# Layer 0 of a four-layer graph network: the reciprocal softmax sums reach the query axis by a VectorE block transpose and transfers through DRAM instead of a TensorE product

## The chip, the cores and the metric

The kernel runs on one core of a Trainium2 chip. A core has TensorE (PE: products; its weight loads are listed as PEld), VectorE (DVE), ScalarE (ACT), GpSimd (POOL), SyncE (SP, which here only starts transfers) and 16 DMA engines. The metric is device time in microseconds of one launch; a case's time is the median over runs.

## The reference

Four layers on 4096 nodes with 256 features, each followed by a residual sum and a layer norm over the features. `adj` is 4096 x 4096, under 1% filled.

```python
# layer 0: four heads of 64
qkv = x @ Wqkv + bqkv
scores = einsum('hnd,hmd->hnm', qh, kh) * SCALE + graph_bias * adj
scores = where(adj == 0, -1e9, scores)
attn = softmax(scores, axis=-1)
x = layernorm(x + (attn @ vh) @ Wout + bout)
# layer 1: graph attention, softmax over leaky_relu(e_src + e_dst), masked
# layer 2: normalised adjacency @ x @ W.T + b;  layer 3: the same form, then relu
```

The change concerns the softmax of layer 0 alone: its division by the row sums.

## The kernel before

Layer 0 works on blocks of 128 query rows (`Rows`, 32 of them), and in each on two pairs of heads (`Pair`), so 64 pairs ("units"). The 4096 keys of a pair are taken in four steps of 1024. A step is written out by hand in `step(t)`: every engine gets its instructions in that order, and three units are in flight at different stages.

In one step, `t`, and for the units that are at that point:

- `score` (L366): TensorE writes scores of both heads into two PSUM tiles `sc`, 128 queries on the partitions, 1024 keys along. VectorE adds the bias and the mask, takes the row maximum and writes `z` (L375). There is one `sc` tile for each head, so the next step's scores wait until VectorE has read them.
- `expo` (L391), one unit (four steps) later: ScalarE takes the exponential of `z` with the row maximum subtracted, and accumulates the row sums into `ls`, one column for each step.
- `turn` (L405, L413), one step after that: TensorE transposes `z` in pieces into PSUM (`ptr`), ScalarE copies it to `pt`, keys now on the partitions.
- `attend` (L423), one step later still: TensorE accumulates values times `pt` into `po`, over the four steps. `po` is 128 x 128: the two heads' 64 features on the partitions, the queries along. It takes one of two PSUM buffers by turns.

Because `po` has the queries along its columns while the sums have them on the partitions, one reciprocal for each query and head must be laid along the columns, the same for the 64 partitions of its head. `sums` (L434 to L437), in the third of a pair's four attending steps, adds the four partial sums, takes the reciprocal and copies each along 64 columns (`lb`, 128 x 128). `norm` (L441 to L449), in the fourth, multiplies `lb` as the stationary operand with the identity on TensorE, which gives `lb` transposed in PSUM (`pb`), and VectorE copies it to `rb`. `scale` (L452), at the head of the next step, multiplies `po` by `rb` into `oT`; on VectorE it stands ahead of that step's two `z`. After a second pair, `finish` (L335 to L348) multiplies `oT` with the output weights, adds the residual and takes the layer norm's statistics.

Beside this, VectorE builds the next block's bias from the adjacency (`make_bias`: `rt` L272, `u` L277, `bias` L278), and ScalarE and GpSimd keep a bf16 copy of it (`make_edges`: `mk` L289; on a diagonal piece two small GpSimd operations L293, L294; GpSimd starts the transfer to `edge` in DRAM, L295). `mk` has two buffers. The query projection of the next block (`begin`: `pq` L313, and GpSimd's addition to `xr`, L329) stand in the step that begins with a second pair's `scale`. SP starts the loads of `raw` (L256), `xq` and `xr`.

Each engine works through its own instructions in order, and a wait stops all that stands behind it on that engine. GpSimd's starts of transfers are such instructions too.

Of the kernel before, what the change touches and what calls it, by code (L numbers as in the profile page):

```python
# [8 lines left out]
F32 = mybir.dt.float32  # L9
# [7 lines left out]
P = 128  # L17
# [3 lines left out]
HD = D // H  # L21
NCH = N // P
# [4 lines left out]
NS = N // TS  # L27
# [3 lines left out]
QB = P // NA  # L31
# [13 lines left out]
def tile_gnn(  # L45
# [18 lines left out]
    nc = tc.nc  # L64
# [8 lines left out]
    dram = ctx.enter_context(tc.tile_pool(name="dram", bufs=1, space=DRAM))  # L73

    ident = const.tile([P, P], F32, name="ident")
# [29 lines left out]
    sc = [ps_q.tile([P, TS], F32, name=f"sc{j}") for j in range(2)]  # L105

    edge = dram.tile([N, N], BF16, name="edge")
    off_diag = const.tile([P, P], F32, name="off_diag")
    nc.vector.tensor_scalar(off_diag, ident, -1.0, 1.0, ALU.mult, ALU.add)

# [58 lines left out]
    with ExitStack() as l0:  # L169
        ps_t = l0.enter_context(tc.tile_pool(name="l0ps_t", bufs=1, space=PSUM))  # L170
        ps_o = l0.enter_context(tc.tile_pool(name="l0ps_o", bufs=1, space=PSUM))
# [5 lines left out]
        wk2 = l0.enter_context(tc.tile_pool(name="l0work2", bufs=2))  # L177
# [26 lines left out]
        def project(mb):  # L204

            xt = x_in.pop(mb)
            for pr in range(2):
                pk = ps_o.tile([P, 512], F32, tag=f"po{pr}", name="pk")
                for cc in range(2):
                    nc.tensor.matmul(  # L210
                        pk,
                        wkv_sb[:, cc, pr * P : (pr + 1) * P],
                        xt[:, cc, :],
                        start=(cc == 0),
                        stop=(cc == 1),
                    )
                nc.scalar.activation(
                    kT[:, pr, mb * 512 : (mb + 1) * 512],
                    pk,
                    AF.Identity,  # L220
                    bias=bqk_sb[:, 2 + pr : 3 + pr],
                )
            pv = ps_t.tile([P, 4, D], F32, tag="tr", name="pv")
            for s in range(4):
                for cc in range(2):
                    nc.tensor.matmul(  # L226
                        pv[:, s, :],
                        xt[:, cc, s * P : (s + 1) * P],
                        wkv_sb[:, cc, D : 2 * D],
                        start=(cc == 0),  # L230
                        stop=(cc == 1),
                    )
            nc.vector.tensor_tensor(
                v_sb[:, mb * 4 : (mb + 1) * 4, :],
                pv,
                bv_b.unsqueeze(1).to_broadcast([P, 4, D]),
                ALU.add,
            )
            if mb + 4 < N // 512:
                load_x(mb + 4)  # L240
# [109 lines left out]
        class Pair:  # L350
# [79 lines left out]

            def sums(self):

                l2 = wk2.tile([P, 2], F32, tag="l2", name="l2")
                nc.vector.tensor_reduce(l2, self.ls, AX.X, ALU.add)  # L434
                nc.vector.reciprocal(l2, l2)
                self.lb = wk2.tile([P, 2, HD], F32, tag="lb", name="lb")
                nc.vector.tensor_copy(self.lb, l2.unsqueeze(2).to_broadcast([P, 2, HD]))  # L437

            def norm(self, tag):
                pb = ps_o.tile([P, 512], F32, tag=tag, name="pb")  # L440
                nc.tensor.matmul(  # L441
                    pb[:, 0:P],
                    self.lb.rearrange("p j d -> p (j d)"),
                    ident,
                    start=True,
                    stop=True,
                )
                self.rb = wk2.tile([P, P], F32, tag="rb", name="rb")
                nc.vector.tensor_copy(self.rb, pb[:, 0:P])  # L449

            def scale(self):
                nc.vector.tensor_tensor(  # L452
# [4 lines left out]
        pairs = {}  # L457
# [4 lines left out]
        def step(t):  # L462
            unit, k = divmod(t, NS)
            ib, pr = divmod(unit, 2)
            live = t < n_steps
            ua, ka = divmod(t - LA, NS)
            tag_a, tag_o = f"po{ua % 2}", f"po{1 - ua % 2}"
            ut, kt = divmod(t - LT, NS)
            ue, ke = divmod(t - LE, NS)
            attends = 0 <= ua < n_units  # L470
            turns = 0 <= ut < n_units
            expos = 0 <= ue < n_units
            grow = live and ib + 1 < NCH
            if grow and pr == 0 and k == NS - 1:
                rows[ib + 1].fetch()
            if ua > 0 and ka == 0:
                pairs[ua - 1].scale()
            if t > 0:
                for mb in range(2 * t, min(2 * t + 2, N // 512)):
                    project(mb)  # L480
            if live:
                if k == 0:
                    pairs[unit] = Pair(rows[ib], pr)
                pairs[unit].score(k)
            if expos:
                pairs[ue].expo(ke, 0)
            if turns:
                pairs[ut].turn(kt, 0)
            if expos:
                pairs[ue].expo(ke, 1)  # L490
            if attends:
                pairs[ua].attend(ka, tag_a)
                if ka == NS - 2:
                    pairs[ua].sums()
                if ka == NS - 1:
                    pairs[ua].norm(tag_o)
            if ua > 0 and ka == 1:
                if ua % 2 == 0:
                    pairs[ua - 1].rows.finish(tag_o)
                del pairs[ua - 1]  # L500
            if grow:
                if pr == 1 and k == NS - 2:
                    rows[ib + 1].begin(tag_o if attends else "po1")
                kb, half = divmod(pr * NS + k, 2)
                if edges:
                    edges.pop().make_edges()
                edges.append(rows[ib + 1])
                rows[ib + 1].make_bias(kb, half)
                if half == 0 and kb + 1 < NS:
                    rows[ib + 1].load(kb + 1)  # L510
                elif half == 0 and ib + 2 < NCH:
                    rows[ib + 2].load(0)
            elif edges:
                edges.pop().make_edges()
            if turns:
                pairs[ut].turn(kt, 1, by_dve=not live)
            for f, *args in tail.get(t, ()):
                f(*args)

# [131 lines left out]
        with tc.manual_schedule():  # L651
            load_x(0)
            nc.sync.dma_start(wkv_sb, wqkv[:, D:].rearrange("(c p) e -> p c e", p=P))
            rows[0].load(0)
            load_x(1)
            rows[0].load(1)
            rows[0].fetch()
            load_x(2)
            load_x(3)
            nc.scalar.dma_start(wout_sb, wout.rearrange("(c p) e -> p c e", p=P))  # L660
            nc.scalar.dma_start(bout_b, bout.partition_broadcast(P))
            rows[0].begin("po1")
            for k in range(NS):
                for half in range(2):
                    rows[0].make_bias(k, half)
                    rows[0].make_edges()
                if k < 2:
                    project(k)
                if k + 2 < NS:
                    rows[0].load(k + 2)  # L670
                elif k + 2 == NS:
                    rows[1].load(0)
            for t in range(n_steps + LA + 2):
                step(t)
# [5 lines left out]
    with ExitStack() as l1:  # L680
        wk = l1.enter_context(tc.tile_pool(name="l1work", bufs=2))
        pp_ = l1.enter_context(tc.tile_pool(name="l1pt", bufs=2))
        ps_o = l1.enter_context(tc.tile_pool(name="l1ps_o", bufs=2, space=PSUM))
# [166 lines left out]
    with ExitStack() as l2:  # L850
# [173 lines left out]
        with tc.manual_schedule():  # L1024
            prepare(0, 0)
            sums(0)
            prepare(1, 0)
            blk = None
            for t in range(n_all):
                layer, tl = divmod(t, T1)  # L1030
                jb, c = divmod(tl, NP)
# [4 lines left out]
                if t + 1 < n_all:  # L1036
                    sums(t + 1)
# [8 lines left out]
                if c == NP - 1:  # L1046
# [8 lines left out]
                    for s in range(NSJ):  # L1055
                        p = jb * NSJ + s
# [65 lines left out]
```

## Time and profile before

| | us |
|---|---|
| runs, median of 3 | 2810.7 (2809.99 to 2813.46) |
| profiled execution | 2810.3 |
| its span, first to last instruction | 2808.5 |
| TensorE busy | 2740.4 (98%) |
| VectorE busy | 2234.3 (80%) |
| ScalarE busy | 1615.1 (58%) |
| GpSimd busy | 234.2 (8%) |

Layer 0 fills about the first 1435 us of the span, layer 1 ends near 1990, and layers 2 and 3 fill the rest. The kernel-wide shares are means over these stages. A row of the list of groups reads: line, engine, operation, output <- inputs, shapes and count, then busy time in all and mean duration in ns of one, then the engine's idle time just before these instructions and what ended it. Instructions on TensorE overlap, so what one adds is read from the chain that ended last, in which each piece is what the next had to wait for.

### The profile page before, as it was taken

The numbers are of one execution on the slowest core, as the hardware profiler recorded it, in microseconds if no ns is written. First come the engines' busy times: TensorE is split into PE (matmuls) and PEld (weight loads), VectorE is DVE, ScalarE is ACT, GpSimd is POOL, SyncE is SP. The second block draws the span as 40 slices with busy tenths as digits, with TensorE's granted clock in tenths as the row PEclk, the third lists the DMA queues.
The fourth block names the chain that finished last, engine by engine and source line by source line (L and its number), as shares of the span: only waits on it lengthen the run. The fifth ranks groups of instructions, "written<-read, shape, count | busy, mean of one in ns | idle before, by whom it ended". The sixth has DMA issues, their size and how long they took to land.

```text
span 2808.5 us, 58032 instructions
## 1 busy us (share of the span) xinstructions
PE 2740.4 (98%) x23664; PEld 1870.2 (67%) x23664; DVE 2234.3 (80%) x4091; ACT 1615.1 (58%) x2483; POOL 234.2 (8%) x404
## 2 busy tenths in 40 slices
PE   6999999999999999999998999999999999999997
PEld 4677777777777777777777888887444444444443
DVE  4799999999898999999758888885876568666565
ACT  2699999999999999999855655653100001000000
POOL 1111111111111111111100000000200000000000
PEclk9999999999999999999998999999999999999999
DMA  6344444444444444444362222212555545555552
GB/s 157 61 86 85 87 92 85 88 86 88 90 87 82 90 91 82 86 92 89 100 188 68 76 73 70 76 46 72 177 157 173 163 154 163 164 160 179 180 169 76
DMA packets 671291, 308.01 MB, mean 110 GB/s; under 512 B 547376, under 2 KB 577456, under 8 KB 671024
## 3 DMA queue, kind: packets, MB, share of 16 engines
q1 hardware_dynamic: 655776, 265.10, 38.4%
q0 software_dynamic: 13440, 37.77, 3.5%
q8 instruction: 185, 3.03, 0.5%
q10 hardware_dynamic: 1808, 1.44, 0.2%
q14 instruction: 82, 0.67, 0.1%
HBM read 258.21 MB, written 46.01 MB: 108 GB/s over the span
## 4 chain that ended last, share of the span: by engine, by line
PE 96%; DVE 2%; ACT 1%; DMA 1%; issue 1%; SPq 0%; DVEq 0%; ACTq 0%
PE m L950 27%; PE po L423 17%; PE po L775 16%; PE sc L366 16%; PE ptr L405 10%; PE py L984 2%; PE pq L313 1%; PE pp L335 1%; PE pb L441 1%; PE pk L210 1%; PE pv L226 1%; PE sc L137 1%; PE pm L744 0%; SPq L256 0%; DMA xt<-in_xT 0%
## 5 line engine op out<-in xcount | busy, mean ns | idle before, releaser
L375 DVE CUSTOM_DVE_ANT_0 z<-sc,bias 128x1024 f32<-128x1024 f32 x512 | 605.8, 1220 | 40.5 <-PE sc L366 38.9
L391 ACT ACTIVATE z<-z,nm 128x1024 f32<-128x1024 f32 x512 | 590.2, 1153 | 6.7 <-DVE nm L387 6.7
L413 ACT COPY pt<-ptr 128x1024 f32<-128x1024 f32 x507 | 511.3, 1008 | 99.2 <-PE ptr L405 89.3
L366 PE MATMUL sc<-store,qT 64*128 64x512 f32 x2048 | 507.0, 608 | 1.4 <-DVE mx L375 1.3
L423 PE MATMUL po<-pt,xc 128*64 128x128 f32 x8192 | 504.1, 276 | 0.0
L775 PE MATMUL po<-store,pt 128*128 128x257 f32 x2048 | 459.5, 382 | 3.6 <-DVE pt L765 3.6
L423 PEld LDWEIGHTS po<-pt,xc 128*64 128x64 f32 x8192 | 442.1, 137 | 17.6 <-DVE pt L411 0.2
L405 PEld LDWEIGHTS ptr<-ident,z 64*128 64x128 f32 x8192 | 322.3, 138 | 177.6 <-issue 78.4
L775 PEld LDWEIGHTS po<-store,pt 128*128 128x128 f32 x2048 | 385.0, 190 | 62.9 <-issue 3.6
L950 PE MATMUL m<-asum,ysum 128*128 128x512 f32 x768 | 357.0, 595 | 6.3 <-issue 6.3
L405 PE MATMUL ptr<-ident,z 64*128 64x64 f32 x8192 | 356.5, 225 | 5.8 <-ACT pt L413 4.4
L366 PEld LDWEIGHTS sc<-store,qT 64*128 64x128 f32 x2048 | 192.9, 189 | 119.7 <-issue 109.4
L950 PEld LDWEIGHTS m<-asum,ysum 128*128 128x128 f32 x768 | 146.1, 190 | 177.9 <-issue 160.2
L950 PE MATMUL m<-asum,store 128*128 128x512 f32 x512 | 263.1, 596 | 0.0
L724 ACT ACTIVATE z<-z,es_q 128x1024 f32<-128x1024 f32 x128 | 147.1, 1149 | 183.2 <-DVE mx L711 178.9
L950 PE MATMUL m<-a,ysum 128*128 128x512 f32 x512 | 245.3, 592 | 0.0
L295 POOL DMA_DIRECT2D edge<-mk x256 | 145.3, 568 | 1004.5 <-ACT mk L289 981.0
L956 ACT COPY e<-m 128x512 f32<-128x512 f32 x32 | 18.5, 586 | 351.3 <-PE m L950 351.3
L919 DVE TENSOR_TENSOR asum<-a 128x512 f32<-128x512 f32 x128 | 88.0, 687 | 163.7 <-PE m L950 163.7
L278 DVE SCALAR_TENSOR_TENSOR bias<-rt,gb,u 128x512 f32<-128x512 f32 x256 | 194.1, 758 | 9.1
L950 PEld LDWEIGHTS m<-asum,store 128*128 128x128 f32 x512 | 97.8, 191 | 123.6 <-issue 121.9
L272 DVE STREAM_TRANSPOSE rt<-raw 128x512 f32<-128x512 f32 x256 | 179.6, 702 | 0.0
(126 smaller groups left out, 2544.5 us busy)
## 6 DMA issues: line engine op xcount, KB each, us to landing
a<-in_adjT SPq DMA_DIRECT2D x256, 512.0 KB, 5.1
raw<-in_adjT SPq DMA_DIRECT2D x512, 128.0 KB, 3.9
edge<-mk POOLq DMA_DIRECT2D x256, 128.0 KB, 2.5
mk<-edge SPq DMA_DIRECT2D x256, 128.0 KB, 2.9
xt<-in_xT SPq DMA_DIRECT2D x8, 512.0 KB, 5.3
xq<-in_xT SPq DMA_DIRECT2D x32, 128.0 KB, 3.8
xr<-in_x SPq DMA_DIRECT2D x32, 128.0 KB, 3.0
x<-xs POOLq DMA_DIRECT2D x8, 512.0 KB, 4.0
```

Of the source, the lines that this page charges most:

```text
L272: nc.vector.transpose(rt.rearrange("p (b r) -> p b r", r=QB), self.raw_now[:, half * nb : (half + 1) * nb, :],)
L278: nc.vector.scalar_tensor_tensor(self.bias[k][:, m0 : m0 + HT], rt, gb, u, ALU.mult, ALU.add)
L295: nc.gpsimd.dma_start(edge[self.ib * P : (self.ib + 1) * P, k * TS + m0 : k * TS + m0 + HT], mk)
L366: nc.tensor.matmul(ps[j][:, q * 512 : (q + 1) * 512], self.rows.qT[j * HD : (j + 1) * HD, self.pr, :], kT[j * HD : (j + 1) * HD, self.pr, ...
L375: nc.vector.tensor_tensor_reduce(z, ps[j], self.rows.bias[k], 1.0, NEG, ALU.add, ALU.max, self.mx[:, j, k : k + 1],)
L391: nc.scalar.activation(z, z, AF.Exp, bias=self.nm[:, j : j + 1], accum_out=self.ls[:, j, k : k + 1],)
L405: nc.tensor.transpose(pa[:, r, c, :], z[half, c * P : (c + 1) * P], ident[half, half])
L413: nc.scalar.copy(to, pa)
L423: nc.tensor.matmul(self.po[j * HD : (j + 1) * HD, 0:P], v_sb[:, ci, h * HD : (h + 1) * HD], self.pt[j][k][:, c, :], start=(ci == 0), stop= ...
L724: nc.scalar.activation(self.z[s], self.z[s], AF.Prelu, bias=self.eq[:, s : s + 1], alpha=SLOPE)
L775: nc.tensor.matmul(self.po[:, 0 : D + 1], self.pt[:, b, :, :].rearrange("p s i -> p (s i)"), wh[:, b, :], start=(b == 0), stop=(b == NBK - 1),
L950: nc.tensor.matmul(self.m[i], left, right, start=(c == 0), stop=(c == NP - 1))
```

## The change

`sums` now ends with a VectorE transpose in blocks of 32 x 32: the two reciprocals of each query are repeated to 32 columns, and after the transpose each block of 32 partitions holds head 0's 32 reciprocals on its even rows and head 1's on its odd rows. For each head GpSimd then starts a transfer of one row from each of the four blocks (four rows of 128 bytes) into a new DRAM tensor `norm`. A new function, `spread`, at the end of the same step, has GpSimd start two transfers that read 512 bytes each into 64 partitions of `rb`. The old `norm` function, with the TensorE product and the copy out of PSUM, is gone, and so is its call in the fourth attending step. `scale` is unchanged and reads `rb`.

```diff
+    norm = dram.tile([2 * NCH, 2, P], F32, name="norm")
             def sums(self):
+                u = 2 * self.rows.ib + self.pr
                 l2 = wk2.tile([P, 2], F32, tag="l2", name="l2")
                 nc.vector.tensor_reduce(l2, self.ls, AX.X, ALU.add)
                 nc.vector.reciprocal(l2, l2)
-                self.lb = wk2.tile([P, 2, HD], F32, tag="lb", name="lb")
-                nc.vector.tensor_copy(self.lb, l2.unsqueeze(2).to_broadcast([P, 2, HD]))
-
-            def norm(self, tag):
-                pb = ps_o.tile([P, 512], F32, tag=tag, name="pb")
-                nc.tensor.matmul(
-                    pb[:, 0:P],
-                    self.lb.rearrange("p j d -> p (j d)"),
-                    ident,
-                    start=True,
-                    stop=True,
-                )
+                lt = wk2.tile([P, QB], F32, tag="lt", name="lt")
+                nc.vector.transpose(lt, l2.unsqueeze(1).to_broadcast([P, QB // 2, 2]))
+                for j in range(2):
+                    nc.gpsimd.dma_start(
+                        norm[u, j, :].rearrange("(a c) -> a c", c=QB),
+                        lt.rearrange("(a r) c -> a r c", r=QB)[:, j, :],
+                    )
+
+            def spread(self):
+                u = 2 * self.rows.ib + self.pr
                 self.rb = wk2.tile([P, P], F32, tag="rb", name="rb")
-                nc.vector.tensor_copy(self.rb, pb[:, 0:P])
+                for j in range(2):
+                    nc.gpsimd.dma_start(
+                        self.rb[j * HD : (j + 1) * HD, :], norm[u, j, :].partition_broadcast(HD)
+                    )
...
                 if ka == NS - 2:
                     pairs[ua].sums()
-                if ka == NS - 1:
-                    pairs[ua].norm(tag_o)
...
             if turns:
                 pairs[ut].turn(kt, 1, by_dve=not live)
+            if attends and ka == NS - 2:
+                pairs[ua].spread()
```

The order of instructions that results: on VectorE the transpose takes the place of the copy `lb`, and the copy `rb` is gone. On GpSimd the two starts of writes stand ahead of the same step's `edge` transfer, and the two starts of reads behind it, each behind a wait for its write to have landed. `scale` waits for both reads and for `po`.

## The prediction

> **What bounds the kernel now.** I read the chain that ended last first, then busy time by stretch, then the same chain in order of time, then the groups of the touched lines, the order of work around one turn of the sums, and the transfers.
>
> ```profile
> PE m L950 27%; PE po L423 17%; PE po L775 16%; PE sc L366 16%; PE ptr L405 10%; PE py L984 2%; PE pq L313 1%; PE pp L335 1%; PE pb L441 1%; PE pk L210 1%; PE pv L226 1%; PE sc L137 1%; PE pm L744 0%; SPq L256 0%; DMA xt<-in_xT 0%
> ```
>
> The product that goes, `pb`, is itself on the chain, at 1%. In the middle of layer 0 (columns: PE, PEld, DVE, ACT, POOL busy, then clock, DMA share, GB/s):
>
> ```profile
> 500.00:700.00 200.00, 200.00 (x2848) 150.99 (x2844) 183.07 (x357) 186.92 (x309) 30.65 (x54) 1.00 0.44 88
> ```
>
> TensorE has no gap; ScalarE (93%) and VectorE (92%) are close behind. The chain in order of time, around one `pb`:
>
> ```profile
> 635.55 1.77 PE sc L366 x8
> 637.32 0.49 PE ptr L405 x16
> 637.81 1.90 PE po L423 x32
> 639.71 0.42 PE pb L441 x2
> 640.13 0.64 PE ptr L405 x16
> 640.77 1.77 PE sc L366 x8
> ```
>
> A step without `pb` is 1.77 + 0.49 + 1.90 + 0.64 = 4.80 us; this one is 5.22, longer by the 0.42 of `pb`. So the product is paid in full, once for each of 64 head pairs. A block of 128 rows (two pairs, eight steps) takes 41.58 us.
>
> The groups concerned:
>
> ```profile
> L441 PE MATMUL pb<-ident,lb 128*128 128x128 f32 x128 | 31.2, 326 | 0.0
> L449 DVE COPY rb<-pb 128x128 f32<-128x128 f32 x64 | 18.7, 292 | 21.0 <-PE pb L441 18.1
> L437 DVE COPY lb<-l 128x128 f32<-128x128 f32 x64 | 14.5, 227 | 2.2
> L295 POOL DMA_DIRECT2D edge<-mk x256 | 145.3, 568 | 1004.5 <-ACT mk L289 981.0
> ```
>
> POOL is nearly idle: it waits for ScalarE's `mk`. The tightest turn, that of a first pair:
>
> ```profile
> 615.56 0.15 DVE L434 TENSOR_REDUCE l<-ls 128x2 f32<-128x8 f32 x1
> 615.95 0.23 DVE L437 COPY lb<-l 128x128 f32<-128x128 f32 x1
> 616.36 0.54 POOL L295 DMA_DIRECT2D edge<-mk  x1 [5.32 <-ACT mk L289]
> 620.53 0.29 DVE L449 COPY rb<-pb 128x128 f32<-128x128 f32 x1
> 622.60 0.28 DVE L452 TENSOR_TENSOR oT<-po,rb 128x128 f32<-128x128 f32 x1
> 622.94 1.23 DVE L375 CUSTOM_DVE_ANT_0 z<-sc,bias 128x1024 f32<-128x1024 f32 x1
> ```
>
> `scale` (`oT`) stands 7.04 us after the sum's start, and the `z` behind it empties the two score buffers that TensorE fills again in the next step. That gap must hold the new transfers. Nearest rows for them:
>
> ```profile
> edge<-mk POOLq DMA_DIRECT2D x256, 128.0 KB, 2.5
> x_pre<-xr SPq DMA_DIRECT2D x31, 128.0 KB, 2.0
> ```
>
> **What the Trainium skill says.** (1) "DMA: Bandwidth & Descriptors", section on the anatomy of one DMA on the SWDGE (gpsimd) path: about 2.0 us fixed plus bytes/436e3, mostly the write's receipt. The trace agrees: `edge` is 2.2 at the least and 2.5 in the median, the formula gives 2.3. (2) The same page, "Two DMAs through the same engine are not ordered": a dependent transfer must be issued after the first one's semaphore, so two fixed costs add. Nothing in this trace depends so on a POOL transfer within a step. (3) "SBUF — State Buffer", "Who interferes with whom": VectorE in a two-port mode and GpSimd lock each other out of a shared port pair. The trace agrees: `u` (L277) takes 426 ns, and 1456 where POOL's `xr` addition lies beside it; the `edge` issue goes from 542 to 692 ns beside `u`.
>
> **The change part by part.**
>
> TensorE: minus one fp32 product for each pair, 0.42 us on the chain x 64 = 26.9 us. The 0.42 is a difference of steps, so weight loads and start-up are in it. Nothing is added on TensorE.
>
> VectorE: minus `lb` 0.23 and `rb` 0.29, minus the wait for `pb` (21.0/64 = 0.33). Plus one transpose of 128x32: the rows for 512 and 1024 columns are 0.70 and 1.24, so 1.04 ns a column over 0.17; at 32 columns 0.20. Bounds: 0.17 to 0.23 (no dearer than `lb`). VectorE is 0.3 cheaper for each pair, and is not the bound, so I count nothing for it.
>
> POOL: plus four DMA issues for each pair. Its order becomes: two writes (wait for the transpose), `edge` of that step (waits for `mk`), two reads (each waits for its write to land), next `edge`. An issue costs 0.54 (L295); with fewer rows I take 0.5, bounds 0.3 and 0.7: 4 x 0.5 x 64 = 128 us on an engine busy 234 of 2808. Behind the writes waits `edge`, 1.1 us later than now: ScalarE needs that `mk` buffer two steps later (9.6 us), the transfer lands in 2.5 to 3.2, so that is free. Behind the reads waits the next `edge`, whose `mk` comes at 5.3 us; they are out before. At the end of layer 0 POOL's `x` stores start at 1437.8, some 8 us after the last pair's reads would. SP's queue gets nothing. About 64 KB of reads for each pair is nothing beside 88 GB/s at 44% share.
>
> The new wait: `scale` waits for both reads, and behind it on VectorE stand `z` for both heads and thereby TensorE's next scores. From the sum's start (0): sum, reciprocal and transpose to 0.60; POOL notices 0.28 later, as it does after `mk` (616.07 to 616.35): 0.88; writes issued at 0.88 and 1.40. A tiny write is not in the trace. From below 1.7 us (16 engines begin to report 1.8 after an `edge` issue), from above 3.2 (mean of `edge` where the raw loads run); I take 2.2, the least `edge`: 3.1 and 3.6. Reads issued at 3.2 and 3.7, 2.2 to 2.5 each: last one at 5.9 to 6.2.
>
> When is it needed? Without `rb` and its wait, the `z` pair that ends at 620.38 is followed by 1.91 us of `rt`, `u` and `bias`, so `scale` would come at 622.29, 6.73 after the sum's start. Half a microsecond of cover. A further 0.3 is free: in the step at 615.59 `z` starts 0.46 later than usual and TensorE loses 0.16. Past 7.0 us each microsecond of lateness is a microsecond of TensorE. The raw loads start at 6.0 in this phase, just after the reads. In a second pair the same chain is due at about 6.9, and the step after it has 1.1 us of query projection ahead of the next scores, so it has cover to about 8.4. The last pair's `scale` stands 2 us ahead of the output product; its lateness is hidden by the `ped` products.
>
> Other removals: the PSUM turn of `po` tags loses one user, and no product waited for it; nothing counted. Layers 1 to 3 are untouched and start earlier.
>
> Sum: the profiled span 2808.5 - 26.9 = 2781.6. The profiled execution was 2810.3 (1.8 outside the span), so 2783.4; the median of the runs is 0.4 higher: **2784**.
>
> **Rivals.**
>
> A, *the round trip is late, slower.* Place: `scale` of the first pairs, then of all. If each transfer takes 3.2 instead of 2.2 to 2.5, the writes land at 4.6, `rb` at 7.9, and the block loses about the 0.84 that it gained: that is the break-even. With 3.4 it is 8.3: first pairs lose 1.3, second ones still nothing, so 32 x (1.3 - 0.84) = +15 us, about 2826. For it: `edge` has means of 3.1 to 3.9 where raw loads run. Against: from 2 to 6 us after a first pair's sum the DMA engines are idle, and the tiny packets ask little of them.
>
> B, *part of the gain is eaten.* ScalarE's 186.9 of 200 us is 38.9 for a block, 4.86 a step, against plain steps of 4.80, of which there are now six, not four, in eight. If they fell to ScalarE's pace, 6 x 0.06 x 32 = 11 us are lost: 2795. Or the new issues meet `u` at the port pair and delay it by up to 0.4, which costs about 0.16 a step as measured above, 5 to 10 us: 2789 to 2794. For it: the engines are this close. Against: ScalarE's first copy of a step still waits for `ptr`.
>
> C, *no change*: the step is really held by ScalarE, and `pb` fills time in which TensorE would wait: 2811. Against: the `pb` step is longer by exactly `pb`.
>
> **How the numbers follow.** Forecast as worked out, own range 2779 to 2792: 0.70. B: 0.14, 2793 to 2805. C: 0.04. A: 0.09. Better than 2779 (the 0.16 at 615.59 goes as well, 5 us): 0.03. Within 0.2% (5.6 us) is what a measurement cannot tell from no change. Faster 0.70 + 0.14 + 0.03 = 0.87; same 0.04; slower 0.09. The range leaves out A, C, the far end of B and the best case, just under 0.2: 2779 to 2801.
>
> **What would show it.** Right: the first pairs' period and the second's each shorter by 0.42, a block at about 40.7 us, no `pb` on the chain, no idle VectorE time ahead of `oT`, writes landing in about 2 us, and the last read by 6.2 after the sum. Wrong: VectorE idle ahead of `oT` released by `rb`'s transfer, with score products waiting for `mx`; `ptr` waiting for ScalarE in plain steps; `u` far above 0.43; POOL issues well above 0.5.

## The result: no change that can be measured

Over twelve runs each, the kernel after takes 2812.76 us (2808.79 to 2819.4) and the kernel before 2812.5 (2809.99 to 2816.28): a ratio of 1.0004, 95% interval 0.9995 to 1.0013. The profiled execution took 2810.95 us with a span of 2808.9, against 2810.3 and 2808.5. The forecast was 2784, so about 29 us of expected gain are missing.

**The product is gone, as said.** The chain that ended last, by line, for the kernel after:

```profile
PE m L956 27%; PE po L781 16%; PE po L425 16%; PE sc L368 15%; PE ptr L407 10%; PE py L990 2%; PE pq L315 1%; PE pp L337 1%; PE pk L212 1%; PE pv L228 1%; DVE z L377 1%; PE sc L139 1%; DMA rb<-norm 1%; SPq L258 0%; PE pm L750 0%
```

No `pb` stands in it. In its place are VectorE's `z` and the new transfer `rb<-norm`, 1% each. The same chain in order of time (start, duration, what), around a pair's fourth attending step, in which `pb` used to stand behind `po`:

```profile
636.74 1.77 PE sc L368 x8
638.51 0.49 PE ptr L407 x16
639.00 1.90 PE po L425 x32
640.90 0.64 PE ptr L407 x16
641.54 1.77 PE sc L368 x8
```

From scores to scores this step is 4.80 us; with `pb` it was 5.22. Where `rb` came in time, the whole period of a pair (from its first `z` to the first `z` of the next pair) is 18.85 us after a first pair and 21.89 after a second, against 19.27 and 22.31 before: exactly 0.42 less each.

**But TensorE now has gaps.** Busy time in two stretches of layer 0 (columns: length; PE, PEld, DVE, ACT, POOL busy, each with its instructions; then clock, DMA share, GB/s):

```profile
300.00:500.00 200.00, 197.36 (x2752) 147.89 (x2750) 172.26 (x342) 181.22 (x302) 51.89 (x91) 0.98 0.43 86
500.00:700.00 200.00, 200.00 (x2868) 152.14 (x2866) 177.75 (x353) 188.14 (x313) 51.70 (x90) 1.00 0.46 93
```

In the first, TensorE stands for 2.6 us and its clock falls to 0.98. In the second it is busy throughout, since instructions on it overlap and a wait of some tenths shows only as fewer of them: 2868 in the trace against 2888 in the same stretch of the run without these waits (first experiment below). The groups of the touched lines show which engine waits first:

```profile
L297 POOL DMA_DIRECT2D edge<-mk x256 | 143.9, 562 | 586.6 <-ACT mk L291 572.1 <-POOL mk L296 8.9 <-ACT pt L415 2.7
L443 POOL DMA_DIRECT2D norm<-lt x128 | 74.7, 586 | 290.0 <-DVE lt L441 287.1 <-issue 2.8
L453 POOL DMA_DIRECT2D rb<-norm x128 | 69.3, 544 | 64.7 <-DMA norm<-lt 49.4 <-issue 15.2
L458 DVE TENSOR_TENSOR oT<-po,rb 128x128 f32<-128x128 f32 x64 | 18.4, 288 | 45.0 <-DMA rb<-norm 39.7 <-PE ptr L407 2.9 <-PE sc L368 2.3
L441 DVE STREAM_TRANSPOSE lt<-l 128x32 f32<-128x32 f32 x64 | 13.5, 212 | 2.4 <-DVE l L438 0.3
```

VectorE stands idle for 45.0 us ahead of `scale` (`oT`), 39.7 of it until the transfer into `rb` lands. And TensorE waits in turn. The waits of the body of layer 0 (120 to 1345 us: sum, times, longest):

```profile
DVE oT L458 <- DMA rb<-norm: 25.1, 17, 4.4
...
PEld sc L368 <- DVE mx L377: 12.3, 16, 2.7
...
PE sc L368 <- DVE mx L377: 4.7, 4, 2.6
```

The score products wait for `mx`, which VectorE writes with `z` behind `scale`. One late turn in order of time, that of a first pair (start, duration, engine, line, operation, and in brackets the idle time before it and what ended it):

```profile
616.11 0.16 DVE L437 TENSOR_REDUCE l<-ls 128x2 f32<-128x8 f32 x1
...
616.76 0.21 DVE L441 STREAM_TRANSPOSE lt<-l 128x32 f32<-128x32 f32 x1 [0.30 <-DVE l L438]
...
621.87 0.43 DVE L279 TENSOR_SCALAR u<-rt 128x512 f32<-128x512 f32 x1
622.34 0.75 DVE L280 SCALAR_TENSOR_TENSOR bias<-rt,gb,u 128x512 f32<-128x512 f32 x1
624.29 0.29 DVE L458 TENSOR_TENSOR oT<-po,rb 128x128 f32<-128x128 f32 x1 [1.21 <-DMA rb<-norm]
624.50 1.22 DVE L377 CUSTOM_DVE_ANT_0 z<-sc,bias 128x1024 f32<-128x1024 f32 x1
```

`bias` is done at 623.1, 7.0 us after the sum began; `rb` comes 8.1 after it, and `z` follows 1.2 late.

**How often.** In 35 of the 64 pairs `scale` waits at most 0.15 us. In the other 29 it waits by the trace for 44.9 us in all. The table sorts them by what the trace shows late in each (pairs are counted from 0, so even numbers are first pairs). Its last column says by how much the period in which that `scale` stands is longer than in the run without these waits (first experiment below); for the last two blocks, all that is lost from pair 60 to the end of layer 0:

| what was late | pairs | VectorE idle, us | TensorE lost, us |
|---|---|---|---|
| GpSimd standing still for 2.8 to 2.9 us | 14, 29, 44, 59 | 12.2 | 11.0 |
| the second write landing in 3.2 to 3.7 us | 2, 12, 22, 32, 42, 52 | 7.6 | 5.1 |
| reads started 4.3 us after the sum, behind `edge` | 21, 23, 25, 27, 54, 56, 58 | 6.6 | 2.7 |
| a read landing in 3.5 to 4.0 us | 4, 11, 24, 31 | 4.8 | 1.9 |
| the last two blocks, where layer 1's loads begin | 60, 61, 63 | 12.3 | 6.7 |
| small ones | 7, 16, 43, 46, 50 | 1.4 | 0.3 |

In pair 54, the costliest of its row (2.7 us idle, 2.3 lost), the second read also took 4.5 us to land, so its late start is the smaller part.

### The profile page after: what moved, and what is told of

Read it like the earlier page. It is cut to its first block, busy times and chain, and to the rows that moved or that the text cites. A ratio compares the mean times of both kernels' runs of the same rounds, so it can differ in the third digit from the quotient of the medians.

```text
span 2808.9 us, 58279 instructions
## 1 busy us (share of the span) xinstructions
PE 2732.3 (97%) x23536; PEld 1864.5 (66%) x23536; DVE 2193.2 (78%) x4027; ACT 1608.2 (57%) x2483; POOL 378.9 (13%) x660
## 4 chain that ended last, share of the span: by engine, by line
PE 92%; DVE 3%; DMA 2%; issue 1%; ACT 1%; SPq 0%; POOL 0%; DVEq 0%; ACTq 0%; POOLq 0%
PE m L956 27%; PE po L781 16%; PE po L425 16%; PE sc L368 15%; PE ptr L407 10%; PE py L990 2%; PE pq L315 1%; PE pp L337 1%; PE pk L212 1%; PE pv L228 1%; DVE z L377 1%; PE sc L139 1%; DMA rb<-norm 1%; SPq L258 0%; PE pm L750 0%
## 5 line engine op out<-in xcount | busy, mean ns | idle before, releaser
L368 PE MATMUL sc<-store,qT 64*128 64x512 f32 x2048 | 521.7, 608 | 8.3 <-DVE mx L377 8.1
L407 PEld LDWEIGHTS ptr<-ident,z 64*128 64x128 f32 x8192 | 328.8, 138 | 177.1 <-issue 86.3
L407 PE MATMUL ptr<-ident,z 64*128 64x64 f32 x8192 | 366.4, 226 | 4.0 <-ACT pt L415 2.7
L368 PEld LDWEIGHTS sc<-store,qT 64*128 64x128 f32 x2048 | 200.6, 189 | 133.4 <-issue 105.4
```

Of the source, the lines that this page charges most:

```text
L368: nc.tensor.matmul(ps[j][:, q * 512 : (q + 1) * 512], self.rows.qT[j * HD : (j + 1) * HD, self.pr, :], kT[j * HD : (j + 1) * HD, self.pr, ...
L407: nc.tensor.transpose(pa[:, r, c, :], z[half, c * P : (c + 1) * P], ident[half, half])
```

## The experiments

Each was timed together with the kernel before on one chip; ratios are against that, with 95% intervals. "Forecast" below is the 2784 us on record.

### The whole gain, and what takes it away

The first question is whether the removal is worth what was forecast at all, if nobody waits for the new transfers. Two kernels answer it. In one every transfer stays, but `scale` uses the tile of the pair before, which has long landed:

```diff
+                self.rb_old = last_rb[-1] if last_rb else self.rb
+                last_rb.append(self.rb)
...
-                    self.rows.oT[:, self.pr, :], self.po[:, 0:P], self.rb, ALU.mult
+                    self.rows.oT[:, self.pr, :], self.po[:, 0:P], self.rb_old, ALU.mult
```

> The changed kernel with all its transfers, but each scale multiplies by the rb of the pair before, which landed some 15 us earlier (so the normalisation is that of the wrong pair). Theory W (the gain is lost where VectorE waits for rb ahead of z): the wait is gone, so the whole 0.42 us for each pair appears, 2784 to 2788 us, ratio about 0.991. Theory S (the transfers, GpSimd's four more issues and the port pair cost time by themselves): 2800 to 2812, ratio 0.996 to 1.000.

Measured: 2780.62 us (2780.14 to 2785.75), ratio 0.9895 (0.988 to 0.991). In the other the transpose and all four transfers are left out, and a constant tile of ones takes the place of `rb`:

```diff
-                lt = wk2.tile([P, QB], F32, tag="lt", name="lt")
...
-                    self.rows.oT[:, self.pr, :], self.po[:, 0:P], self.rb, ALU.mult
+                    self.rows.oT[:, self.pr, :], self.po[:, 0:P], rb_one, ALU.mult
...
-            if attends and ka == NS - 2:
-                pairs[ua].spread()
```

> The turn of the sums left out: no product, no transpose, no transfer, scale multiplies by a constant 1 (so nothing is normalised). This is the ceiling of what removing the product can bring. Forecast of the prediction: 64 x 0.42 = 27 us, 2784. Theory A (ScalarE takes over as the bound when the product goes): 2795 to 2811. If this is 2784 and the kernel with the old rb as well, the transfers cost nothing but their wait.

Measured: 2784.85 us (2781.21 to 2788.21), ratio 0.9905 (0.9889 to 0.9922). Both lie where the forecast lay. The first one's windows (columns as above) show a TensorE without gaps although GpSimd starts all the transfers:

```profile
300.00:500.00 200.00, 200.00 (x2876) 151.16 (x2872) 179.85 (x353) 189.49 (x316) 53.76 (x94) 1.00 0.44 91
500.00:700.00 200.00, 200.00 (x2888) 152.34 (x2884) 179.05 (x354) 189.28 (x313) 53.91 (x94) 1.00 0.46 94
```

So the transfers as such show no cost, ScalarE does not hold the step, and what the kernel after lost it lost by waiting for `rb`. That the kernel that leaves more out is the slower of the two by 4 us has little to do with layer 0. The first product that stands behind layer 0's output (`sc`, L139 in the kernel after) starts at 1407.8 us in the first run and at 1408.6 in the second, against 1435.0 in the kernel before. The other 3.7 us between the two profiled spans lie behind it, in layers 1 to 3, where the two kernels are alike.

Pair by pair against the first run, the kernel after loses 21.3 us over pairs 0 to 59: 19.3 in first pairs and 2.0 in second ones. What a pair loses follows from when its `rb` lands, in us after the sum's start:

| pair | `rb` lands | TensorE lost |
|---|---|---|
| 16, first | 6.8 | 0.0 |
| 22, first | 7.5 | 0.5 |
| 12, first | 8.3 | 1.3 |
| 54, first | 9.3 | 2.3 |
| 14, first | 10.9 | 7.1 |
| 21, second | 7.7 | 0.0 |
| 59, second | 8.9 | 0.5 |
| 29, second | 9.6 | 1.1 |

A first pair loses what `rb` comes later than 7.0, a second one what it comes later than 8.4. Only 15 of the 60 pairs are past these times, and the rule gives some 17 of the 21.3 us; 3.2 of the rest are pair 14's (last section). From pair 60 to L139 another 6.7 us are lost. Of the 30.2 us between the two spans 2.8 lie in layers 1 to 3; the kernel after was 0.6 ahead at its first sum.

### How much later may `scale` stand

Here `scale` stands behind the two `z` of its step instead of ahead of them, so a late `rb` does not stop the `z` for which the next scores wait:

```diff
-            if ua > 0 and ka == 0:
-                pairs[ua - 1].scale()
...
                 pairs[unit].score(k)
+            if ua > 0 and ka == 0:
+                pairs[ua - 1].scale()
```

> The changed kernel with scale moved on VectorE from ahead of the step's two z to behind them: 2.4 us more for rb to arrive, nothing else. Theory W: of the pairs that were late in the profile of the changed kernel only those late by over 2.4 us (7 of 64, four of them in the last block) still wait, and they wait where TensorE has its next scores already; 2785 to 2792 us, ratio 0.990 to 0.993. Theory S: no better than the changed kernel, 2808 to 2813.

Measured: 2800.39 us (2800.05 to 2801.61), ratio 0.9962 (0.9947 to 0.9977): some 11 us won, not the 19 to 26 expected. The waits in the body of layer 0:

```profile
PEld pq L315 <- DVE oT L458: 16.4, 30, 1.1
...
PE pq L315 <- DVE oT L458: 9.1, 30, 0.9
...
DVE oT L458 <- DMA rb<-norm: 1.7, 1, 1.7
```

The waits for `rb` have gone from 25.1 us to 1.7. But in place of them the query projection `pq` waits in each of 30 blocks, because it needs the PSUM buffer that `scale` of the second pair frees. The period in which a second pair's `scale` stands grows from 21.89 us to 22.24 in the median, some 11 us in all. So the later place is free for first pairs alone.

### The standstills

GpSimd's own timeline in the kernel after, at pair 14 (columns as in the turn above):

```profile
405.70 0.59 POOL L443 DMA_DIRECT2D norm<-lt  x1 [5.41 <-DVE lt L441]
409.06 0.58 POOL L443 DMA_DIRECT2D norm<-lt  x1 [2.78 <-issue]
409.64 0.57 POOL L297 DMA_DIRECT2D edge<-mk  x1
410.20 0.61 POOL L453 DMA_DIRECT2D rb<-norm  x1
412.30 0.53 POOL L453 DMA_DIRECT2D rb<-norm  x1 [1.49 <-DMA norm<-lt]
```

Between the two writes GpSimd waits 2.78 us for nothing that the profile shows ("issue"). It had started 128 transfers; the same happens after 249, 370 and 491, every 121. If it came with the number of GpSimd's instructions, more of them would move it. So sixteen tiny fills are added for each pair:

```diff
                         self.rb[j * HD : (j + 1) * HD, :], norm[u, j, :].partition_broadcast(HD)
                     )
+                for i in range(16):
+                    nc.gpsimd.memset(pad[:, i : i + 1], 0.0)
```

> The changed kernel with 16 tiny memsets on GpSimd for each pair, behind the two reads. The changed kernel's GpSimd stands still for about 3 us with nothing to wait for at 409, 722, 1034 and 1344 us: every 15 pairs, which is every 232 to 236 GpSimd records, or every 120 of its transfers. Theory F (it waits for its next instructions to be fetched, a fixed number at a time): now about 33 records a pair instead of 16, so a standstill every 7 to 8 pairs. Theory R (the ring of transfers is refilled): still every 15 pairs. Time 2805 to 2820 either way.

Measured: 2816.19 us (2810.36 to 2819.97), ratio 1.0012 (1.0005 to 1.0019). GpSimd's timeline there:

```profile
405.62 0.59 POOL L443 DMA_DIRECT2D norm<-lt  x1 [5.41 <-DVE lt L441]
408.98 0.58 POOL L443 DMA_DIRECT2D norm<-lt  x1 [2.77 <-issue]
```

The standstill is at the same transfer, the 129th, and so are the later ones, with about a thousand more instructions on the engine. It goes with the transfers that GpSimd starts. The kernel before had it too, at its 114th and its 220th transfer, 106 apart, but there nobody waited. The first of them:

```profile
621.32 0.69 POOL L295 DMA_DIRECT2D edge<-mk  x1 [4.42 <-ACT mk L289]
629.13 0.55 POOL L295 DMA_DIRECT2D edge<-mk  x1 [7.12 <-ACT z L391]
```

The `mk` of the second row was ready at 626.3, so 2.86 us of its 7.12 are the standstill; the label names something long done. What GpSimd does in it, no run shows.

### The reads behind `edge`

Second candidate for the tail: GpSimd starts the reads only after that step's `edge`, which waits for `mk` and, on the diagonal pieces, for two GpSimd operations. Here the reads come directly behind the writes:

```diff
                     pairs[ua].sums()
+                    pairs[ua].spread()
...
-            if attends and ka == NS - 2:
-                pairs[ua].spread()
```

> The changed kernel with one part of its order undone: the two reads stand on GpSimd ahead of the step's edge transfer (and of its two operations on a diagonal piece), not behind. In the profile of the changed kernel 9 pairs have their reads issued 0.4 to 1.0 us late for that reason (21, 23, 25, 27, 51, 54, 56, 58, 26). Theory W: those rb land at 6.3 instead of 7.2, worth 0.2 to 0.6 us each, 3 to 5 us in all: 2805 to 2809, ratio 0.998. A theory in which the tail comes from GpSimd's own work as a whole expects more, 2790 to 2800; the standstills stay, spaced by 121 transfers.

Measured: 2808.37 us (2805.11 to 2816.62), ratio 0.9994 (0.9987 to 1.0001). Against the kernel before that is 2.5 us better than the kernel after, and the intervals overlap. It fits the table above: of the 6.6 us of VectorE's idle time in that row TensorE lost 2.7, since four of the seven are second pairs, which have cover. So this is not what the kernel after fails by; standstills, slow writes and the last two blocks remain.

### Another queue for the transfers

With the reads placed so, SP starts all four transfers instead of GpSimd:

```diff
-                    nc.gpsimd.dma_start(
+                    nc.sync.dma_start(
                         norm[u, j, :].rearrange("(a c) -> a c", c=QB),
...
-                    nc.gpsimd.dma_start(
+                    nc.sync.dma_start(
                         self.rb[j * HD : (j + 1) * HD, :], norm[u, j, :].partition_broadcast(HD)
```

> As the kernel with the reads first, but all four transfers are started by SP, whose loads for the next rows begin only 6 us after a first pair's sum. By the 2.0 us of the store from SP in the kernel before against 2.5 from GpSimd, rb should land at about 5 us. Theory W with the GpSimd path at fault (standstills, 0.28 us to notice, 0.59 to issue): nearly all pairs are in time, 2784 to 2790, ratio 0.990 to 0.992, and GpSimd's standstills are as in the kernel before (every 107 transfers). If SP is held by its own loads or the delay is in the DMA engines whoever starts the transfer: 2800 or more.

Measured: 2792.57 us (2790.48 to 2796.3), ratio 0.9929 (0.9914 to 0.9944). The first write starts 0.63 us after the sum's start instead of 0.89, the reads at 2.2 and 2.8 to 3.0, and only four pairs are late. The waits in the body of layer 0 show what is paid for it:

```profile
DVE rt L274 <- DMA raw<-in_adjT: 16.2, 15, 1.8
...
DVE oT L458 <- DMA rb<-norm: 0.7, 3, 0.4
```

The 0.7 us was 25.1. But SP also starts the loads of `raw`, and they now stand behind two waits for writes to land: VectorE's `rt` waits for late `raw` fifteen times. The median is just outside the 2784 to 2790 expected.

### A version with cover on every side

The next kernel keeps GpSimd for the transfers and lengthens the time between sum and `scale`: reads first as above; first pairs' `scale` behind `z`; second pairs' `sums` at the head of the step.

```diff
-            if ua > 0 and ka == 0:
+            if ua > 0 and ka == 0 and ua % 2 == 0:
                 pairs[ua - 1].scale()
+            if attends and ka == NS - 2 and ua % 2 == 1:
+                pairs[ua].sums()
...
                 pairs[unit].score(k)
+            if ua > 0 and ka == 0 and ua % 2 == 1:
+                pairs[ua - 1].scale()
...
                 if ka == NS - 2:
-                    pairs[ua].sums()
+                    if ua % 2 == 0:
+                        pairs[ua].sums()
+                    pairs[ua].spread()
```

> The changed kernel with cover put where it is free: reads ahead of the edge transfer, first pairs' scale behind the step's two z, second pairs' sums ahead of the third step's two z (each 2.4 us more, and no query projection kept waiting, which cost the kernel with every scale moved 0.3 us a block). Theory W: only the pairs late by over 2.4 us remain, one or two in the body and the last block: 2784 to 2789, ratio 0.990 to 0.992, better than both. If moving the sums ahead of z holds TensorE up, second pairs' periods grow by up to 0.5 us: 2795 to 2802.

Measured: 2794.67 us (2790.11 to 2798.63), ratio 0.9933 (0.9916 to 0.9949). That is 16 us less than the kernel before, but not the 2784 to 2789 expected. In the body three `oT` still wait for `rb`, 5.8 us in all, the longest 2.9: they are the standstills, at pairs 14, 29 and 44, longer than the cover. The last pair's waits some 5 us more.

The last one adds to this that SP starts the writes, and the writes alone. They wait only for VectorE, so SP's loads stand behind no landing, and GpSimd starts two transfers fewer for each pair:

```diff
-                    nc.gpsimd.dma_start(
+                    nc.sync.dma_start(
                         norm[u, j, :].rearrange("(a c) -> a c", c=QB),
```

> As the kernel with more cover, but SP starts the two writes; GpSimd keeps the two reads, so SP never waits for a landing (with all four on SP, VectorE waited 16 us for late raw loads). From the earlier runs: writes start at 0.63 and land some 1.6 us later, rb lands at about 5.5. Theory W: no late pair in the body but those at a GpSimd standstill, which come at other pairs since GpSimd starts 6 transfers a pair, not 8; the last pair's reads stay slow. 2786 to 2792, ratio 0.991 to 0.993. If it is no better than 2794.7, what is left is not the length of the chain.

Measured: 2784.82 us (2783.34 to 2786.46), ratio 0.9904 (0.9888 to 0.9921). It computes all that the kernel before does, and takes as long as the kernel that leaves the turn out. Its waits:

```profile
DVE z L377 <- PE sc L368: 43.2, 118, 1.0
...
PEld sc L368 <- DVE mx L377: 0.5, 2, 0.2
DVE oT L458 <- DMA rb<-norm: 0.3, 1, 0.3
```

Now VectorE's `z` waits for TensorE's scores 118 times (67 in the kernel after), and TensorE for `mx` twice. A standstill at 1325 us fell where it cost nothing; the last pair's `rb` came 7.1 us after its sum, not 10.5.

## Why the prediction was wrong, by its steps

**TensorE, 0.42 us for each of 64 pairs: right.** Periods are shorter by 0.42, and with no wait for `rb` the product behind layer 0's output (L139) starts 27.2 and 26.4 us earlier than in the kernel before, against 26.9.

**VectorE and GpSimd prices: right or nearly.** The transpose takes 0.21 us (0.20 taken), a write's start 0.59 and a read's 0.54 (0.5 taken, bounds 0.3 and 0.7). The writes start at 0.89 and 1.48 (0.88 and 1.40). `u` takes 0.43 and never more than 0.52 (25 of them took up to 1.46 in the kernel before), so the port-pair half of rival B did not come, and the ScalarE half and rival C fall with the first experiment.

**The cover, and "past 7.0 us each microsecond of lateness is a microsecond": right.** First pairs lose nothing up to 7.0 and second pairs nothing up to 8.4, both as written, and past that what they are late. Pair 14 alone lost much more, 7.1 us for 3.9, and the prediction had no term for that.

**The step that failed is the arrival, "last one at 5.9 to 6.2", taken for every pair.** It set one landing of 2.2 for a write and 2.2 to 2.5 for a read, and did so 64 times. Only 13 of the 64 pairs had `rb` by 6.2. The median is 6.6, 26 pairs are past 7.0, and the slowest first pair of the body has it at 10.9. So a cover of half a microsecond was enough for most pairs and not for 15 of the first 60, which lost nearly all of the 21.3 us. The text had 3.2 us as the far bound of a landing. With that for the second write and 2.5 for its read, `rb` is at 1.4 + 3.2 + 0.1 + 2.5 = 7.2, past 7.0. That belonged in the sum as a share of the pairs. Instead rival A took it as all first pairs or none, at 9 in 100. Rival A's wait is what happened, and the first sign of being wrong, VectorE idle ahead of `oT` and score products waiting for `mx`, is what the trace shows.

**GpSimd's standstill was put at nothing.** It cost 11.0 of the 21.3 us. Two of them stand in the trace of the kernel before, where its waits list an `edge` that waits for ScalarE's `z`, twice, 7.1 us at the longest; 2.9 us of each are the standstill.

**Two agreements are luck.** The 13 early pairs have `rb` at 5.9 to 6.2 since two errors cancel: a write lands in some 1.6 us where it is not disturbed (2.2 taken), and GpSimd starts the read 0.53 after the landing (0.1 taken). And the measured time is that of rival C, "no change", without its mechanism: some 27 us were won and as much was lost.

**Three smaller steps failed with it.** "Reads issued 3.2, 3.7": on seven pairs of the body they stood behind an `edge` and started at 4.3; I had asked who waits for `edge`, not what `edge` waits for. "From 2 to 6 us after a first pair's sum the DMA engines are idle": fetches of instructions run there (below), and a read that comes late meets the raw loads, which start at 6.0. "Its lateness is hidden by the `ped` products", of the last pair: its `scale` was 4.4 us late, and TensorE stood behind `ped`:

```profile
1427.73 2.83 PE L599 MATMUL ped<-xt,w_ed 128*32 128x128 f32 x96
1433.33 2.04 PE L337 MATMUL pp<-wout_sb,oT 128*128 128x256 f32 x4 [2.77 <-DVE rowsum L344]
```

`rowsum` stands on VectorE right behind `oT`. In the kernel before `pp` came without a wait and took 1.13, so 3.7 of the 4.4 us were not hidden.

## What to carry to other kernels

A product on the bounding engine can be traded for a chain of transfers only where the slack exceeds the chain's slow cases, not its usual one: count how many of the pairs lie past the due time, and price each. Then ask of each queue in the chain what else stands on it, before and behind the new instruction, and split the chain so that a wait for a landing never stands ahead of loads. Where the order allows, buy slack first (here by moving one VectorE instruction behind two others and the sum ahead of them), since it absorbs every cause at once.

## What the runs showed of the hardware

**GpSimd stands still for 2.8 to 2.9 us** after every 121 transfers in the mix of `edge`, writes and reads, and after 106 where all are `edge`. It follows the transfers, not the engine's instructions. That it is the engine making room for descriptors is a guess.

**Small transfers are slower while instructions are fetched.** The page of the kernel after lists these fetches as a queue of their own:

```profile
q8 instruction: 184, 3.01, 0.4%
```

That is 16.4 KB a packet. The Trainium skill, "Runtime: NRT & Kernel Launch", section "Instruction fetch mechanics", says that an engine's instruction memory is refilled in blocks of 16 KiB by a DMA queue of its own; the packets agree. In layer 0 most came 8 to 10 us apart and took 0.9 to 1.3 us. A second queue of the same kind, `q14`, has 86 smaller packets, which count as fetches here too. Of the writes of the first 59 pairs, 41 had a fetch in flight between half a microsecond after their start and their landing; they landed in 2.24 us in the median, at most 3.72. The other 77 landed in 1.63, at most 2.42. The six slow second writes of the table are those of every tenth pair, and the same pairs were slow in the runs with `scale` later and with the added fills. The slow reads of the table's fourth row, and pair 54's, had a fetch in flight too. This is a correlation; no run moved the fetches. The Trainium skill, "DMA: Bandwidth & Descriptors", section "Anatomy of one DMA — SWDGE (gpsimd) path", gives 2.0 us fixed plus the bytes. An estimate from it is 2.0 for these writes of 512 bytes, where 1.63 was measured with no fetch in flight, and 2.1 for reads of 32 KB, where 2.38 was.

**A stall of 2.6 us costs TensorE twice.** The windows of the kernel after around pair 14's stall (columns as in the first windows; the clock is the number ahead of the last two):

```profile
415.00:418.00 3.00, 0.65 (x2) 0.29 (x2) 2.13 (x4) 2.12 (x4) 0.54 (x1) 1.00 0.85 178
418.00:421.00 3.00, 2.98 (x12) 1.06 (x11) 2.93 (x6) 0.00 (x0) 0.00 (x0) 0.72 0.00 0
421.00:424.00 3.00, 3.00 (x29) 2.60 (x29) 2.75 (x7) 1.56 (x2) 0.00 (x0) 0.50 0.01 3
424.00:427.00 3.00, 3.00 (x38) 2.45 (x36) 0.89 (x2) 1.47 (x5) 1.34 (x3) 0.64 0.42 67
```

TensorE waits 2.6 us, until 417.35; from 419 its clock is granted half, for 6.8 us. Half of that is 3.4; with the 3.9 us by which pair 14's `rb` was past 7.0 that makes 7.3, and the period was longer by 7.1. The Trainium skill, "TensorE: Matmul & The Clock Gate", section "What's actually happening", has half speed come after an idle window of some 3.4 us; here 2.6 us of standing were enough. The shorter stalls of the other late pairs in the body of this kernel, up to 0.9 us, did not do it. In between no threshold shows: half speed followed a stall of 1.6 us in the run with the reads first, at 1043, and did not follow one of 2.1 in the kernel after, at 1371.
